# Three memsets of GpSimd between its indirect transfers, in a one-core kernel of a macaron network with a mixture of experts

## The chip, the core and the metric

The kernel runs on one core of a Trainium2 chip. A core has four engines that compute, each with its own queue of instructions that it works off in order: TensorE (PE in the profile; its weight loads are shown apart as PEld), VectorE (DVE), ScalarE (ACT) and GpSimd (POOL). SyncE (SP) issues plain DMA transfers. Transfers whose rows are picked by a list of indices (indirect transfers) are issued by GpSimd, which also makes their descriptors. Engines wait for each other through semaphores: an instruction counts one up when it is done, another waits until it has reached a value.

The metric is the time of one run on the device in microseconds. Three runs of the kernel before took 1364.46, 1364.88 and 1371.0 us; the median is 1364.88.

## What is computed

The reference has two layers around a stream `x` of four sequences of 512 positions with 128 features, all in fp32:

```python
x = L0_attn_x                                   # (4, 512, 128)
x = x + 0.5 * L0_ffn(layernorm(x))              # ternary-weight FFN, 512 hidden
x = x + L0_attn(layernorm(x))                   # a state-space recurrence (Mamba), 256 channels x 16 states
x = x + 0.5 * L0_ffn(layernorm(x))
x = x + 0.5 * L1_ffn(layernorm(x))              # mixture of experts: 64 experts, 8 for each row
x = x + L1_attn(layernorm(x))                   # causal attention, 8 heads, one key/value head
x = x + 0.5 * L1_ffn(layernorm(x))
```

The mixture of experts is what the change touches:

```python
rw = route(x)                                   # 8 experts of 64 for each row, with weights
expert_out = silu(x @ Wg[e].T) * (x @ Wu[e].T) @ Wd[e].T      # for every expert e
out = sum_e rw[:, e] * expert_out[e] + shared_mlp(x)
```

## The kernel before

**Stages.** The four sequences are called blocks. First come the two ternary FFNs and the recurrence of every block (about 400 us of the profile). Then follow the mixture of experts, attention, and the mixture of experts once more. In a mixture of experts two blocks form a group, and a group goes through three steps:

- *send* (L1065): the router picks 8 experts for each row. Every row is then written 8 times to the buffer `sent` in DRAM, sorted by expert. A scatter (L1147) writes one of the 8 copies of 128 rows of 512 bytes; a block takes 4 x 8 = 32 scatters (L1126 to L1128), a group 64.
- *by_tiles* (L1165): `sent` is read back in tiles of 128 rows that have one expert each, four tiles in a batch. TensorE transposes them, multiplies by the expert's weights, and SyncE writes the result to `back` in DRAM. 24 batches are always done; a rest that only some inputs need stands behind a branch (L1254), which all engines pass together.
- *take* (L1291): a gather (L1156) fetches one of the 8 results of 128 rows into a tile `y`. Again there are 32 in a block and 64 in a group. VectorE multiplies each by its weight and adds it to `total`. TensorE transposes the sum and VectorE adds it to `x`.

With four groups (two for each of the two mixtures) there are 256 scatters and 256 gathers. Two tiles `y` of 8 slices each are in use by turns, so a batch of gathers can run 16 ahead of VectorE.

**What sets the order.** Nothing is issued as the code is read. Every instruction is recorded as an `Op`, and a planner (`schedule`, L446) plays the engines through with costs for each instruction (`costs`, L380) and ranks, and puts out one order for each engine, which `issue` (L529) then writes out. For a scatter or gather the planner counts `INDIRECT` (L54) microseconds on GpSimd, and 6 more until the rows have landed (L418):

```python
        if op.name in ("scatter", "gather"):
            return INDIRECT, INDIRECT + 6.0
```

**What the change touches.** `issue` writes a small memset of GpSimd ahead of an operation that has the mark `apart`. Scatters have this mark (L1154): it says that scatters into the same buffer never write the same row, so that no wait is put between them. Gathers don't have it. The memset is `between` (L627), which writes 8 numbers of one partition of a tile `scratch` that nothing reads:

```python
    scratch = fixed.tile([1, 8], F32, tag="scratch", name="scratch")
    plan.between = lambda: real.gpsimd.memset(scratch, 0.0)
```

The planner doesn't know of these memsets; they are written out behind its back. Waits on semaphores are added by the framework, which sees that two memsets write the same tile.

Of the kernel before, what the change touches and what calls it, by code (L numbers as in the profile page):

```python
# [50 lines left out]
GROUPS = ((0, 1), (2, 3)), ((0, 1), (2, 3))  # L51
MOST = {n: ((n * S * TOPK + E * (P - 1)) // P + 3) // 4 * 4 for n in (1, 2)}
OFTEN = {2: 96, 1: 72}
INDIRECT = 1.25  # L54
READ = 4
PART = 11

# [221 lines left out]
class Plan:  # L279
# [100 lines left out]
    def costs(self, op):  # L380
# [36 lines left out]
        if op.name in ("scatter", "gather"):  # L417
            return INDIRECT, INDIRECT + 6.0  # L418
        if op.eng == "gpsimd":
# [26 lines left out]
    def schedule(self):  # L446
# [23 lines left out]
        while todo:  # L470
# [23 lines left out]
            t, op = best  # L494
            ready[op.eng].remove(op)
            issue, length = self.costs(op)
            if op.eng == "scalar":
                s = self.table(op)
# [8 lines left out]
            if op.eng == "tensor" and t > clock["tensor"] + 0.05:  # L507
                t += 0.1
            op.at, op.free_at, op.end = t, t + issue, t + length
            if op.eng == "sync":  # L510
                pipe = max(pipe, op.free_at) + length
# [17 lines left out]
    def issue(self, order):  # L529
        def real(x):  # L530
            return x.real() if isinstance(x, View) else x

        data = mybir.DependencyInfo(mybir.DependencyClass.Sync, mybir.DependencyReason.DATA)
        apart = {}

        def past(ins, op):
            for name in apart.get(op.past, ()):
                self.tc.add_manual_dep(ins.ins, name, data, reason="all rows")

        with self.tc.manual_schedule():  # L540
            for op in order:
                if op.go:
                    if op.apart:

                        self.between()
                    if op.name == "branch":
                        op.go(lambda ins: past(ins, op))
                        continue
                    ins = op.go()
                    if op.apart:  # L550
                        if op.apart in apart:
                            self.tc.declare_no_dep(ins.ins, group=op.apart, reason="no two rows are the same")
                        self.tc.add_to_no_dep_group(op.apart, ins.ins)
                        apart.setdefault(op.apart, []).append(ins.ins.name)
                    continue
                if getattr(op, "switch", False) and self.table(op) == "exp":
                    self.nc.scalar.preload_act_table_set("natural_log_exp_and_others")
                ins = getattr(getattr(self.nc, op.eng), op.name)(  # L558
                    *(real(x) for x in op.args), **{k: real(x) for k, x in op.kw.items()}
                )  # L560
                past(ins, op)
# [985 lines left out]
```

## Time and profile before

| | |
|---|---|
| median of three runs | 1364.88 us |
| the profiled execution, in whole | 1659.86 us |
| its span, on which all views of the profile stand | 1658.0 us |
| granted clock of TensorE in it | 0.856 |
| busy: PE, DVE, ACT, POOL | 1213.3, 986.4, 636.8, 550.2 us |
| 256 gathers on POOL (L1158) | 243.9 us, 953 ns each |
| 256 scatters on POOL (L1149) | 277.7 us, 1085 ns each |
| 256 memsets of `scratch` (L627) | 95 ns each at the median |

The profiled execution is 295 us longer than the runs that are timed; durations are read from it, and the time that counts is that of the runs. In a row of the timeline the first number is the start in us from the span's start, the second the length in us, then come engine, line, operation, what is written and read, and in brackets how long the engine had been idle and what ended that ("issue" is time in which it waited for nothing that the profile shows). Rows of an indirect transfer on POOL show the making of its descriptors; the landing of the rows is not in them. Operations that the planner writes out have the line of the helper that issues them (L558), so they are told apart by their tiles. In a table of windows each row has the stretch, its length, the busy time of each engine with its instructions, the granted clock, the share of the DMA engines and GB/s.

### The profile page before, as it was taken

The page shows a single profiled execution, that of the slowest core. Times are in us where ns is not written, and L with a number is a line of the kernel's source. Part 1 is how long each engine was busy: PE and PEld are TensorE (multiplying, and loading weights), DVE is VectorE, ACT ScalarE, POOL GpSimd, SP SyncE. Part 2 cuts the span into 40 slices and gives each one's busy share as a digit, 9 for nine tenths or more (in the row PEclk, how much of TensorE's full clock was granted, in tenths as well). Part 3 has the DMA queues.
Part 4 walks back from the last instruction along what each step waited for, and adds up shares of the span by engine and source line. Part 5 has one row for each costly group of instructions (what it writes and reads, how often), then busy time and mean ns, then how long its engine had stood idle before and what let it go on. Part 6 is the DMA issues. An engine that isn't in the chain of part 4 may idle for free. (4 is left out here: it accounts for less than half of the span.)

```text
span 1658.0 us, 17225 instructions
## 1 busy us (share of the span) xinstructions
PE 1213.3 (73%) x5006; PEld 740.8 (45%) x5006; DVE 986.4 (59%) x2413; ACT 636.8 (38%) x1207; POOL 550.2 (33%) x794
## 2 busy tenths in 40 slices
PE   6999989999897857567697686693964965676600
PEld 4743323334332436457574333351542655566500
DVE  1287899999896636335464567473674563254422
ACT  4776678674543332122243242251432512221200
POOL 0000000002865434434513554307044043345375
PEclk8999999999997978688797889797996986887855
DMA  4366847541306314334321110001011133344321
GB/s 142 103 224 225 277 161 203 185 116 32 87 23 223 110 62 132 92 122 132 115 90 40 38 36 29 26 4 61 7 37 40 39 110 106 121 130 120 117 59 47
DMA packets 74583, 166.72 MB, mean 101 GB/s; under 512 B 17688, under 2 KB 27953, under 8 KB 73361
## 3 DMA queue, kind: packets, MB, share of 16 engines
q1 hardware_dynamic: 58097, 131.89, 25.4%
q0 software_dynamic: 16384, 33.59, 6.7%
q8 instruction: 50, 0.82, 0.2%
q14 instruction: 52, 0.43, 0.1%
HBM read 117.44 MB, written 83.36 MB: 121 GB/s over the span
## 5 line engine op out<-in xcount | busy, mean ns | idle before, releaser
L1158 POOL DMA_INDIRECT y<-back,at x256 | 243.9, 953 | 329.4 <-issue 112.0
L1149 POOL DMA_INDIRECT sent<-xt,at x256 | 277.7, 1085 | 175.4 <-issue 79.4
L558 PE MATMUL bank<-h,h 128*128 128x512 f32 (+1 forms) x576 | 243.3, 565 | 8.5 <-DVE h L558 6.4
L1232 PE MATMUL bank<-gate_up,xc 128*128 x768 | 169.6, 350 | 47.9 <-DVE xc L558 14.6
L558 ACT ACTIVATE hr<-bank 128x176 f32<-128x176 f32 x192 | 59.3, 319 | 296.0 <-PE bank L1232 123.2
L558 PEld LDWEIGHTS bank<-h,h 128*128 128x128 f32 x576 | 108.7, 195 | 129.0 <-issue 112.8
L1232 PEld LDWEIGHTS bank<-gate_up,xc 128*128 128x128 f32 x768 | 136.0, 216 | 63.8 <-issue 31.0
L1232 PE MATMUL bank<-down,hc 88*128 x768 | 137.9, 295 | 27.3 <-DVE hr L558 13.8
L558 PE MATMUL ys<-pt,vo 128*128 128x512 f32 (+3 forms) x256 | 94.4, 488 | 79.7 <-ACT pt L558 56.7
L558 DVE TENSOR_TENSOR hr<-hr,bank 128x176 f32<-128x176 f32 x192 | 62.4, 332 | 133.1 <-ACT hr L558 79.5
L1232 PEld LDWEIGHTS bank<-down,hc 88*128 88x128 f32 x768 | 121.9, 207 | 35.2 <-DVE hr L558 17.0
L558 DVE TENSOR_TENSOR_SCAN hs<-da,hs 128x512 f32<-128x512 f32 (+1 forms) x128 | 132.1, 1074 | 0.2
L558 DVE COPY xc<-bank 128x512 f32<-128x512 f32 x96 | 65.8, 687 | 101.5 <-PE bank L558 58.3
L558 PE MATMUL bank<-ident,xr 128*128 128x128 f32 x384 | 88.7, 297 | 48.1 <-DMA xr<-sent 17.4
L558 ACT ACTIVATE p<-p,a_low 128x256 f32<-128x256 f32 (+3 forms) x128 | 70.8, 554 | 132.6 <-DVE a_low L558 95.7
L558 POOL MEMSET eq<- 128x256 f32 x8 | 2.6, 321 | 357.6 <-DVE gt L558 357.6
L558 PE MATMUL bank<-kt,q 128*128 128x512 f32 (+3 forms) x256 | 88.4, 470 | 39.9 <-DVE q L558 30.3
L558 ACT ACTIVATE h<-bank,vec 128x512 f32<-128x512 f32 (+1 forms) x108 | 67.2, 639 | 111.4 <-PE bank L558 102.7
L558 DVE SCALAR_TENSOR_TENSOR total<-y,by,total 128x128 f32<-128x128 f32 x224 | 77.5, 347 | 51.8 <-DMA y<-back,at 46.9
L558 DVE CUSTOM_DVE_ANT_0 p<-bank,mask 128x512 f32<-128x512 f32 (+3 forms) x128 | 58.9, 486 | 82.6 <-remote 47.6
L558 PEld LDWEIGHTS ys<-pt,vo 128*128 128x128 f32 x256 | 48.4, 208 | 118.0 <-ACT pt L558 64.2
L558 ACT ACTIVATE da<-rep,neg_a 128x512 f32<-128x512 f32 (+1 forms) x160 | 88.7, 625 | 26.5 <-DVE hs L558 24.9
(188 smaller groups left out, 2082.0 us busy)
## 6 DMA issues: line engine op xcount, KB each, us to landing
sent<-zero SPq DMA_DIRECT2D x48, 512.0 KB
xr<-sent SPq DMA_DIRECT2D x96, 256.0 KB
back<-yr SPq DMA_DIRECT2D x96, 256.0 KB
rep<-spread SPq DMA_DIRECT2D x48, 256.0 KB
back<-zero SPq DMA_DIRECT2D x14, 512.0 KB
bc<-kept SPq DMA_DIRECT2D x24, 256.0 KB
rep<-spread SPq DMA_DIRECT2D x32, 128.0 KB
sent<-xt,at POOLq DMA_INDIRECT x256
```

The source lines that it names most:

```text
L558: ins = getattr(getattr(self.nc, op.eng), op.name)(*(real(x) for x in op.args), **{k: real(x) for k, x in op.kw.items()})
L1149: return real.gpsimd.indirect_dma_start(out=rows.real(), out_offset=bass.IndirectOffsetOnAxis(ap=at.real(), axis=0), in_=x.real(), in_offs ...
L1158: return real.gpsimd.indirect_dma_start(out=y.real(), out_offset=None, in_=rows.real(), in_offset=bass.IndirectOffsetOnAxis(ap=at.real(), ...
L1232: return real.tensor.matmul(ps.real(), lhsT=lhs.real(), rhs=w.real()[..., bass.ds(to["at"][j] * n, n)], start=True, stop=True)
```

## The change

Scatters and gathers both get three memsets of `scratch` ahead of them, where scatters had one and gathers none. The planner's cost of an indirect transfer on GpSimd goes from 1.25 to 1.7 us. Since the planner makes the order of all engines from its costs, that order is made anew.

```diff
-INDIRECT = 1.25
+INDIRECT = 1.7
+PACE = 3
...
         with self.tc.manual_schedule():
             for op in order:
                 if op.go:
-                    if op.apart:
-
-                        self.between()
+                    if op.name in ("scatter", "gather"):
+
+                        for _ in range(PACE):
+                            self.between()
                     if op.name == "branch":
                         op.go(lambda ins: past(ins, op))
                         continue
```

## The prediction

> **What bounds the kernel now.** I read the profile from its end. The chain of work that ended last, in order of time, is one repeating pair: a gather on GpSimd (POOL, 0.94 us) and 0.30 us of "issue", until the last gather lands and VectorE adds its rows up. This is the window from 1627.76 us, with rows left out:
>
> ```profile
> 1627.76 0.95 POOL y L1158
> 1628.71 0.30 issue
> 1629.01 0.94 POOL y L1158
> ...
> 1631.51 2.43 DMA y<-back,at
> ...
> 1650.01 0.69 DVE x L558
> ```
>
> The reader is to see that nothing but GpSimd's issue sets the pace there. One landing of 2.43 us shows, once. POOL's own timeline shows where this tail begins, and what stands ahead of it:
>
> ```profile
> 1541.95 0.95 POOL L1158 DMA_INDIRECT y<-back,at  x1 [0.30 <-issue]
> 1567.75 0.94 POOL L1158 DMA_INDIRECT y<-back,at  x1 [24.85 <-SPq L1254]
> 1569.00 0.94 POOL L1158 DMA_INDIRECT y<-back,at  x1 [0.30 <-issue]
> ```
>
> The last batch of 64 gathers starts at 1567.75, after POOL sat idle for 24.85 us waiting for the branch at L1254 (it stands behind the last expert tiles). From start to start a gather takes 1569.00 - 1567.75 = 1.25 us, so the tail is 64 x 1.25 = 80 us. That whole tail is on the path; the other 192 gathers and 256 scatters are issued while TensorE has other work.
>
> A scatter in an undisturbed stretch, from the same view:
>
> ```profile
> 1240.68 0.09 POOL L627 MEMSET scratch<- 1x8 f32 x1
> 1240.98 0.97 POOL L1149 DMA_INDIRECT sent<-xt,at  x1 [0.21 <-issue]
> 1241.95 0.10 POOL L627 MEMSET scratch<- 1x8 f32 x1
> 1242.26 0.97 POOL L1149 DMA_INDIRECT sent<-xt,at  x1 [0.21 <-issue]
> ```
>
> A scatter has one memset ahead of it and a pitch of 1242.26 - 1240.98 = 1.28 us (1.27 at the median of most batches); a gather has none and 1.25. So the first memset costs 0.02 us: it lies inside the 0.30 us that POOL needs between two transfers anyway.
>
> **The change, part by part.** Removed: nothing. Added: scatters go from one memset to three (256 x 2 = 512), gathers from none to three (256 x 3 = 768). The constant moves only where the planner thinks the transfers end.
>
> *One chained memset.* In the built program's order every memset of scratch but the first waits for GpSimd's own count, because the one before writes the same tile. The trace never shows two of them in a row, so I bound the step. Near rows, from the start of POOL's timeline:
>
> ```profile
> 0.25 0.10 POOL L1540 MEMSET const-float32-0.0<- 128x1 f32 x1 [0.25 <-issue]
> 0.28 0.12 POOL L1540 MEMSET const-float32-1.0<- 128x1 f32 x1
> ...
> 1.07 0.20 POOL masks.py:65 MEMSET upper<- 128x128 f32 x1
> 1.32 0.29 POOL masks.py:199 TENSOR_SCALAR_AFFINE_SELECT ident<-ident 128x128 f32<-128x128 f32 x1
> ```
>
> Without a wait, memsets follow each other at 0.03 us. With a wait on POOL's own count (the select), the next starts 0.05 us after the end of the instruction before it (1.07 + 0.20 = 1.27). A memset of scratch lasts 0.095 us, so a step is 0.095 + 0.05 = 0.145 us. At the most each one pays the 0.21 us that a transfer pays after a memset: 0.305. The first of the three hides as today's does (0.02); two steps are added: for a gather 0.02 + 2 x 0.145 = 0.31 us at the near row, 0.63 at the upper end; 0.02 less for a scatter. At the lower end the transfer's 0.30 us of preparation overlaps the waits and about 0.1 is left. I take 0.35, close to the near row (the one measured wait of this kind on this engine) and leaning a little to the planner's own 1.7 - 1.25 = 0.45.
>
> *A rule against a row.* The Trainium skill, GPSIMD Engine Reference, section "Instruction dispatch", says that consecutive Pool instructions are no barrier: the next one starts before the one before has ended everywhere. By this rule three memsets stream at the 0.03 us of the constants' rows, 0.09 us in all, and vanish in the 0.30 us: the sum would be 1365. But the rule speaks of instructions without a semaphore wait between them, and these have one; the select's row decides, and by it the tail grows.
>
> *The tail.* 64 x 0.35 = 22.4 us, all of it on the path, since POOL is never idle there but for its 0.30 us. A second rule speaks against this cost: DMA: Bandwidth & Descriptors, section "Anatomy of one DMA", puts the fixed 2.0 us of such a transfer mostly in the write's receipt and little in its setup, so slower issue would hide under landings. By that, the tail grows by nothing. The row disagrees: landings overlap, the 2.43 us appear once at the end, and 64 pitches of 1.25 us make the length. I go by the row.
>
> *Everything else on POOL* has slack. The batch of gathers before the tail may end 24.85 us later before it delays the tail; it has 64 gathers, so 22.4 us: it fits, barely. The first layer's second batch of gathers ends at 995.7 and the next scatter starts at 1014.2: 18.5 us of slack, so those scatters start 3.9 us later. They and the following batch have 60 and 67 us of idle POOL behind them. The last scatters end at 1385.1, and POOL's next work comes 45.9 us later; 32 x 0.33 = 11 us fits. The first layer's scatters end at 522.4 and 684.7, with 34 and 42 us of slack behind them, against at most 21. Cover gone, this would cost up to 20 us at one place.
>
> *The planner.* It counts 1.7 where it counted 1.25, and so moves VectorE's sums of gathered rows behind more expert work. POOL's order is the same but for one mask memset that comes two scatters earlier. TensorE and VectorE change places of instructions from the first scatters on; no new transfer or queue entry arises. I give this 3 us for the batch that fits barely and either sign of 10 for the shuffle.
>
> **Sum.** 22.4 + 3 = 25 us. The profiled execution took 1659.86 us (span 1658.0), the runs 1364.88 at the median: it is 295 us longer than what is timed. Its own sum would be 1659.86 + 25 = 1685. I carry the 25 us unscaled to the median, as POOL's pitch is its own: 1390 us, 1.8% slower.
>
> **Rivals.** *Pacing frees the other engines (faster).* There are stretches where everything but POOL stands still while scatters run:
>
> ```profile
> core 0: us, PE busy (x) PEld busy (x) DVE busy (x) ACT busy (x) POOL busy (x), PEclk, DMA share, GB/s
> 1144.70:1158.30 13.60, 0.00 (x0) 0.00 (x0) 0.01 (x1) 0.00 (x0) 9.47 (x18) 0.50 0.14 48
> 1233.50:1256.70 23.20, 0.00 (x0) 0.00 (x0) 0.00 (x0) 0.02 (x1) 19.35 (x37) 0.56 0.16 54
> ```
>
> In the second, ScalarE waits 23.93 us for TensorE's count though the matmuls ended at 1232.5. Eight such stretches make 96.9 us. If half of that exists in the timed runs and gaps between transfers let the counts through, it gives 25 - 48 = -23: 1342. It decides from 25 us saved. Against it: these stretches already have a memset and 0.30 us between transfers, and the timed run is 295 us shorter than the profiled one, so most of the stalls can't be in it. Chance 0.10.
>
> *The memsets hide (no change).* The rule above holds and 0.30 us covers all three: 1365. For it: the first one hides. Against it: the wait on POOL's count. Chance 0.12.
>
> *A dear chain (much slower).* Each step is 0.305: the tail gains 64 x 0.63 = 40, the batch before it overruns its 24.85 by 15: 1420. Chance 0.13. For it: a transfer does pay 0.21 after a memset.
>
> **How the numbers follow.** Likeliest (0.65): 1390, its own range 1375 to 1405 from 0.2 to 0.5 us a gather and the shuffle. The range 1360 to 1420 takes in the hidden case and half of the dear one, and leaves out the faster case and the other half: 0.10 + 0.07. About 0.5% (7 us) is what a measurement of this kernel can tell from no change. Faster 0.10 (pacing), same 0.12, slower 0.65 + 0.13 = 0.78.
>
> **What would show it.** In the profile after: pairs of memsets of scratch 0.15 us apart from start to start; a gather pitch of 1.6 and a scatter pitch of 1.6; a last batch of 64 gathers some 100 us long at the end; idle before it shrunk from 24.85 to a few us. Wrong would be: memsets 0.03 apart (no change), steps of 0.3 (dear), or standing stretches gone and a shorter time (pacing).

## The result, and the profile after

The changed kernel takes **1409.47 us** (median of 4 runs, 1406.87 to 1409.97) against 1364.67 us before (4 runs, 1363.49 to 1371.0): a ratio of 1.0306 with an interval of 1.0287 to 1.0325, or 44.8 us more. The forecast was 1390 us and slower, its range 1360 to 1420. Sign and range hold; of the 44.8 us, the forecast had 25.

The profiled execution of the changed kernel took 1406.87 us, the same as its timed runs; the one of before had taken 1659.86 us, far from its own. The two traces can't be laid side by side to see what the change costs: before's is 253 us *longer*. The experiments show what that was (the second and third group below); the stages of the loss are therefore compared with the kernel of the second experiment instead.

The costliest groups of the page after that belong to the change (line, engine, operation, tiles, count, then busy us, mean ns of one, idle time ahead of them):

```profile
L1151 POOL DMA_INDIRECT sent<-xt,at x256 | 267.3, 1044 | 174.8 <-issue 105.2
L1160 POOL DMA_INDIRECT y<-back,at x256 | 245.3, 958 | 71.3 <-issue 37.7
L629 POOL MEMSET scratch<- 1x8 f32 x1536 | 150.4, 98 | 59.3
```

The transfers cost GpSimd what they did before. All that is new there is 1536 memsets instead of 256, with 59.3 us of idle time just ahead of them. (Lines are two further down than before.) GpSimd's timeline of the kernel after, at the last batch of gathers and inside it:

```profile
1289.49 0.95 POOL L1160 DMA_INDIRECT y<-back,at  x1 [0.15 <-issue]
1290.44 0.40 POOL L629 MEMSET scratch<- 1x8 f32 x3
1298.11 0.95 POOL L1160 DMA_INDIRECT y<-back,at  x1 [7.27 <-SPq L1256]
1299.06 0.40 POOL L629 MEMSET scratch<- 1x8 f32 x3
1299.61 0.95 POOL L1160 DMA_INDIRECT y<-back,at  x1 [0.15 <-issue]
...
1309.56 0.40 POOL L629 MEMSET scratch<- 1x8 f32 x3
1310.56 0.95 POOL L1160 DMA_INDIRECT y<-back,at  x1 [0.61 <-DVE total L560]
```

The three memsets end 0.40 us after the first starts. With 0.095 us for one that makes a step of (0.40 - 0.095) / 2 = 0.153 us. The next gather then starts 0.15 us later, so the pitch is 1299.61 - 1298.11 = 1.50 us (it was 1.25). The first gather into a tile `y`, each eighth, takes 0.46 us more. The last two rows show one. In the built program such a gather waits for two counts, VectorE's sums among them, and every other one for a single count.

### The profile page after: what moved, and what is told of

Its sections match the earlier page's. It is cut to its first block, busy times and chain, and to the rows that moved or that the text cites. A ratio compares the mean times of both kernels' runs of the same rounds, so it can differ in the third digit from the quotient of the medians.

```text
span 1405.1 us, 18486 instructions
## 1 busy us (share of the span) xinstructions
PE 1147.9 (82%) x5006; PEld 702.6 (50%) x5006; DVE 982.2 (70%) x2413; ACT 643.8 (46%) x1211; POOL 666.2 (47%) x2074
## 5 line engine op out<-in xcount | busy, mean ns | idle before, releaser
L1151 POOL DMA_INDIRECT sent<-xt,at x256 | 267.3, 1044 | 174.8 <-issue 105.2
L629 POOL MEMSET scratch<- 1x8 f32 x1536 | 150.4, 98 | 59.3
L1234 PE MATMUL bank<-gate_up,xc 128*128 x768 | 149.3, 322 | 3.7 <-DVE xc L560 2.0
L1234 PE MATMUL bank<-down,hc 88*128 x768 | 125.6, 282 | 7.1 <-DVE hc L560 5.6
L1234 PEld LDWEIGHTS bank<-gate_up,xc 128*128 128x128 f32 x768 | 121.2, 195 | 15.6 <-issue 8.3
L1234 PEld LDWEIGHTS bank<-down,hc 88*128 88x128 f32 x768 | 112.7, 196 | 12.4 <-DVE hc L560 4.2
L560 ACT ACTIVATE p<-p,a_low 128x512 f32<-128x512 f32 (+3 forms) x128 | 70.8, 554 | 91.8 <-DVE a_low L560 91.6
L560 PE MATMUL bank<-ident,total 128*128 128x128 f32 x32 | 9.2, 353 | 114.0 <-DVE total L560 113.9
L560 PE MATMUL bank<-kt,q 128*128 128x512 f32 (+3 forms) x256 | 82.9, 444 | 13.8 <-DVE q L560 9.0
L560 ACT COPY yr<-bank 128x512 f32<-128x512 f32 x96 | 56.1, 585 | 81.3 <-PE bank L1234 76.4
```

The costliest lines, as they stand in the source:

```text
L560: ins = getattr(getattr(self.nc, op.eng), op.name)(*(real(x) for x in op.args), **{k: real(x) for k, x in op.kw.items()})
L1151: return real.gpsimd.indirect_dma_start(out=rows.real(), out_offset=bass.IndirectOffsetOnAxis(ap=at.real(), axis=0), in_=x.real(), in_offs ...
L1234: return real.tensor.matmul(ps.real(), lhsT=lhs.real(), rhs=w.real()[..., bass.ds(to["at"][j] * n, n)], start=True, stop=True)
```

## The experiments

The experiments of a group ran side by side on one chip with the kernel before, so each group below has its own time of before (the third has two chips and two such times). After the result I held this: the gap that the wait adds to each transfer costs time in more places than the tail, and the new order gives a part of it back. The rivals were that the order itself is what costs, that the memsets cost as instructions and not by their waits, and that the loss lies in the tail alone.

### First group: one part alone (before 1365.36 us, 1363.55 to 1368.15, 14 runs)

**Memsets without the planner's new cost.**

```diff
-INDIRECT = 1.7
+INDIRECT = 1.25
```

> The three memsets of the changed kernel with the planner's old cost of 1.25 us. Theory A (the memsets are the cost: from the last scatters on, GpSimd is the bound in timed runs, so about 160 to 190 transfers pay 0.25 us each): 1365 + 40 to 48, near the changed kernel's 1409 or a little over. Theory B (only the last 64 gathers pay, 16 to 19 us, and the rest of the 45 us comes from the planner's new order): about 1383. In the profile a gather pitch of 1.50 us in either.

Measured: 1459.32 us, ratio 1.0684 (1.0665 to 1.0703). That is 94 us lost, twice the loss of the whole change and more than was expected.

**The planner's new cost without any added memset** (on the kernel before).

```diff
-INDIRECT = 1.25
+INDIRECT = 1.7
```

> The planner's cost of 1.7 us with the memsets of before (one ahead of a scatter, none ahead of a gather). Theory A: 1365 within 6 us, since the order alone costs nothing. Theory B: 1385 to 1392, since the new order carries some 25 us of the loss. Gather pitch 1.25 us.

Measured: 1349.41 us (1348.74 to 1350.14), ratio 0.9883 (0.9865 to 0.9901): 16 us gained. No kernel of this study is faster where before takes 1365 us; on the other kind of chip (second group) it was not run.

**One memset ahead of every transfer, old cost.**

```diff
-INDIRECT = 1.7
-PACE = 3
+INDIRECT = 1.25
+PACE = 1
```

> One memset ahead of scatters and gathers alike, planner's cost 1.25 us. Both theories: the memset lies inside the 0.30 us between two transfers (0.02 us each), so 1365 to 1369. It also asks what the profile of before did to its run: if it is a memset between gathers that lets the profiled execution run at its timed speed, this one's profiled execution takes about 1370 us; if it takes three, it takes about 1660 as before.

Measured: 1369.51 us, ratio 1.0027 (1.0017 to 1.0037), at a gather pitch of 1.26. A gather's first memset costs about 0.01 us, and 2 to 5 us come out at the end. This kernel has the planner's order of before, and so serves below as a trace of that order in an execution of 1372.02 us.

**Three memsets that don't wait for each other.** Nine tiles are used by turns, so that a memset doesn't write what the one before it wrote.

```diff
-    scratch = fixed.tile([1, 8], F32, tag="scratch", name="scratch")
-    plan.between = lambda: real.gpsimd.memset(scratch, 0.0)
+    scratch = itertools.cycle(
+        [fixed.tile([1, 8], F32, tag=f"scratch{i}", name=f"scratch{i}") for i in range(9)]
+    )
+    plan.between = lambda: real.gpsimd.memset(next(scratch), 0.0)
```

> The changed kernel with its three memsets in turn into nine tiles, so that none waits for the one ahead of it. If the waits between the memsets make their price (theory of the prediction): memsets 0.03 us apart, gather pitch 1.25 to 1.32, time that of the planner's change alone, 1365 to 1375. If a memset costs 0.15 us whether it waits or not: pitch 1.50 and 1409.

Measured: 1353.95 us (1351.01 to 1355.26), ratio 0.9913 (0.9889 to 0.9936). GpSimd's timeline of this run, in the last batch:

```profile
1282.15 0.17 POOL L631 MEMSET scratch<- 1x8 f32 x3
1282.47 0.95 POOL L1162 DMA_INDIRECT y<-back,at  x1 [0.15 <-issue]
1283.42 0.17 POOL L631 MEMSET scratch<- 1x8 f32 x3
1283.74 0.95 POOL L1162 DMA_INDIRECT y<-back,at  x1 [0.15 <-issue]
```

Three memsets take 0.17 us instead of 0.40, and the pitch is 1.27. The same number of instructions on the same engine, without the waits, costs 1353.95 - 1349.41 = 4.5 us; with them it costs 1409.47 - 1349.41 = 60.1. So it is the wait of one memset for the one before that is paid for, not the memset.

**What the four say together.** The order made with 1.7 is worth 16 us when the pitch is 1.25. At the pitch of 1.50, the planner that counts 1.25 loses another 50 us (1459.32 - 1409.47). VectorE shows where. It works off its queue in order, and the planner places the sums of gathered rows in that queue for the time at which it thinks the rows have landed. The view of who waited for whom (total us, times, longest), with the old cost and three memsets:

```profile
DVE total L560 <- DMA y<-back,at: 172.2, 154, 8.7
```

The same row with the old cost and one memset:

```profile
DVE total L560 <- DMA y<-back,at: 94.8, 96, 9.2
```

With three memsets VectorE stands 77 us longer in front of its sums, and all that is queued behind each sum stands with it. The end moves by 1459.8 - 1370.2 = 89.6 us of span. (How much of the 89.6 comes by way of these waits was not measured apart.)

### Second group: which transfers (before 1665.87 us, 1658.82 to 1670.1, 9 runs)

These were meant to tell which batches of transfers carry the cost. On this chip the kernel before took 300 us longer than in the first group, in timed runs.

**The kernel before, once more** (no edit).

> The kernel before, unchanged, profiled once more. If the standing stretches of its first profile belong to that one execution, this one takes about 1365 us under the profiler, and shows how much room really lay behind each batch of transfers: 10 us or less ahead of the last 64 gathers, in place of the 24.85 read before. If they belong to the kernel, it takes about 1660 us again.

Measured: 1663.85 us, and its trace has the standing stretches of the prediction's profile again. The table of windows, for the third batch of scatters of the second mixture (its columns are in the first line, each engine's instructions in brackets):

```profile
core 0: us, PE busy (x) PEld busy (x) DVE busy (x) ACT busy (x) POOL busy (x), PEclk, DMA share, GB/s
1228.30:1269.00 40.70, 8.39 (x44) 6.05 (x42) 10.65 (x38) 6.55 (x19) 34.03 (x63) 0.68 0.18 62
```

And the waits of the same stretch (from 1230 to 1270 us):

```profile
PEld ys L558 <- issue: 31.1, 1, 31.1
PE ys L558 <- issue: 30.8, 1, 30.8
ACT pt L558 <- remote: 30.3, 1, 30.3
```

GpSimd keeps its rhythm, while TensorE stands for 30.8 us, and VectorE and ScalarE with it; the stretch ends at 1268.5, during the last of the 32 scatters. TensorE has a wait there, though its row says "issue": its next matmul reads `pt`, and ScalarE and VectorE write `pt` from a `bank` that TensorE has filled. From the timeline of the same run:

```profile
1236.79 1.20 PE L558 MATMUL bank<-ident,p 128*128 128x128 f32 x8
1237.83 0.49 PE L558 MATMUL bank<-ident,xr 128*128 128x128 f32 x3
...
1268.52 0.58 ACT L558 COPY pt<-bank 128x512 f32<-128x512 f32 x1 [30.26 <-remote]
1269.16 2.08 PE L558 MATMUL ys<-pt,vo 128*128 128x512 f32 x2 [30.84 <-issue]
...
1270.57 0.69 DVE L558 COPY pt<-bank 128x512 f32<-128x512 f32 x1 [31.58 <-remote]
```

The matmuls into `bank` end by 1238.3, and both readers start 30 us later. "Remote" means that a count went up then though no instruction that raises it had just ended. In the packed trace this count is TensorE's own: its last update before the stretch comes at 1236.8 us, the next at 1268.4, while three matmuls that raise it end by 1238.3. So TensorE's work is done, and its count reaches the others late. Over this whole trace 105 of the 1201 recorded updates of that count come more than 1.5 us after the last matmul that raises it, but only 2 of VectorE's 1837 and 2 of ScalarE's 793; in the third experiment's trace it is 2 of TensorE's 1275. Waits ended by "remote" add up (over the engines) to 351 and 393 us in the two profiles of the kernel before, and to nothing in the four traces of the first group and in the changed kernel's of the result.

So the 1659.86 us of the first profile were no fault of that execution alone: on this chip the kernel takes that long in every timed run.

**Memsets in the last 64 gathers alone** (planner 1.7, one memset ahead of scatters).

```diff
+                        gathers += op.name == "gather"
-                        for _ in range(PACE):
+                        for _ in range(1 if op.name == "scatter" else PACE if gathers > 192 else 0):
```

> The planner's cost of 1.7 us (1349 us with the memsets of before), and three chained memsets ahead of the last 64 gathers alone. All of that batch is on the path: 64 x 0.25 and 0.45 more at each eighth, which waits for two counts: 19 us, so 1368. If the price is spread otherwise (the tail hides part behind landings), less than 1360.

Measured: 1656.27 us, ratio 0.9941 (0.9909 to 0.9973). It has the planner's new order as well and gains only 10 us, so the far larger gains of the next two are not that order's.

**Memsets ahead of scatters alone** (gathers have none).

```diff
-                        for _ in range(PACE):
+                        for _ in range(PACE if op.name == "scatter" else 0):
```

> Planner's cost 1.7, three memsets ahead of scatters, none ahead of gathers. By the room that the prediction read (34 to 46 us behind the batches of scatters) nothing: 1349. By the traces after (the experts' first tiles come directly behind the last scatters): 8 to 28 us, so 1357 to 1377.

Measured: 1470.11 us, ratio 0.8832 (0.8795 to 0.8869): 196 us *faster*.

**Memsets ahead of gathers alone** (scatters keep their one).

```diff
-                        for _ in range(PACE):
+                        for _ in range(PACE if op.name == "gather" else 1):
```

> Planner's cost 1.7, three memsets ahead of gathers, one ahead of scatters as before. By the prediction's room: the tail alone, 1368. By the traces after: the tail 19, the batch before it 16 to 18, the first mixture's up to 10: 1384 to 1396. With the scatters' run this should add up to the changed kernel's 60 us over 1349, if batches don't share room.

Measured: 1572.47 us, ratio 0.9441 (0.9409 to 0.9472): 93 us faster. On this chip each kind that is paced gives back standing time, most of all the scatters: the waits ended by "remote" come to 89 us with the scatters paced and 224 with the gathers.

### Third group: the change on such chips

**The changed kernel itself, once more** (no edit; before 1672.02 us here, 1665.89 to 1679.92, 12 runs).

> The changed kernel once more, beside the kernel before on the same chip. The kernel before took 1365 us on one chip and 1665 on another, so the chip decides what is tested. Where before takes 1365: 1409 again. Where before takes 1665 (its engines stand still while transfers are issued at 1.25 us): if the longer gap of the three chained memsets frees them, as it did for scatters and gathers alone (1470 and 1572), both together take 1400 to 1420; if part of the stalls stays, 1450 or more.

Measured: 1432.81 us (1430.5 to 1435.23), ratio **0.857** (0.8549 to 0.859). The same kernel that loses 44.8 us in the result gains 239 us here. The table of windows, for the same batch of scatters as above:

```profile
core 0: us, PE busy (x) PEld busy (x) DVE busy (x) ACT busy (x) POOL busy (x), PEclk, DMA share, GB/s
1058.50:1110.90 52.40, 45.64 (x216) 31.34 (x215) 40.96 (x129) 24.96 (x61) 41.19 (x125) 0.97 0.23 75
```

The batch is 11.7 us longer, and TensorE is busy for 45.64 us in it instead of 8.39, at a granted clock of 0.97 instead of 0.68. With the same planner's order on the same chip but unpaced scatters (the next run) it is busy for 14.37 us in this batch. The waits ended by "remote" come to 14.5 us in the whole trace.

**The tail alone, again** (the edit of the second group, on the chip of the run above).

> Planner's cost 1.7 and three memsets ahead of the last 64 gathers alone. Where before takes 1365, the planner's cost alone gives 1349 and the tail's price is 64 x 0.25 + 8 x 0.45 = 19 us: 1368. Where before takes 1665: 1656 again, as the tail has no other engine's work to free.

Measured: 1672.13 us, ratio 0.9996 (0.9966 to 1.0025), where the last chip had given 0.9941. With such differences between chips, the tail's price can't be read here; it is taken from traces below.

**The unchained memsets and the gathers alone, again** (the edits above; before 1674.56 us, 1672.46 to 1684.63, 7 runs).

> Planner's cost 1.7 and three memsets that don't wait for each other: as many memsets as the changed kernel has, but a gather pitch of 1.27 us, not 1.50. Where before takes 1365: 1354 again. Where before takes 1665: if it is the longer gap between transfers that frees the other engines, they still stand still here and it takes 1640 to 1670; if it is the memsets as such, whatever the gap, it takes 1355 to 1430.

> Planner's cost 1.7, three chained memsets ahead of gathers, one ahead of scatters. Where before takes 1365: by the room that the prediction read, the tail alone, 1349 + 19 = 1368; by the stages of the traces, the tail 19, the batches before it 16 to 18 and the first mixture's up to 10: 1384 to 1396. Where before takes 1665: 1572 again.

Measured: 1641.51 us, ratio 0.979 (0.975 to 0.983), with the unchained memsets; 1596.81 us, ratio 0.9529 (0.9487 to 0.9571), with memsets ahead of gathers. Three memsets that leave the pitch at 1.27 us for gathers and 1.29 to 1.30 for scatters bring little here: their trace has ten standing stretches of 3 to 6 us that the first group's trace of this kernel doesn't have, and 249 us of waits ended by "remote". So it is not the memset as such that frees the engines, but the chained one, with its longer gap between transfers.

**What is shown and what stays open.** On three chips the kernel before takes 1666 to 1675 us in timed runs. The standing time all but goes away when the pitch of the indirect transfers grows from 1.25 (gathers) and 1.27 (scatters) to 1.50 and 1.52 us, and what stands in it are late counts of TensorE. Why these counts are late while GpSimd issues transfers was not found out, nor whether a pitch between 1.30 and 1.50 us would do. In every run the longer gap came with GpSimd's waits for its own count, so the two are not told apart. Each chip was used once, so whether the chip or something else at that time makes the difference is not shown; and on which chip the first profile was taken is not on record. The tail alone, the scatters alone and the gathers alone never ran on a chip without the stretches.

## Why the prediction was right, and where not

All of this is for the result and the first group, where before takes 1365 us. The timed loss is made up as follows. The planner's new order gives 16 us (second experiment: 1365.36 to 1349.41). From there to the changed kernel it is 1409.47 - 1349.41 = 60.1, across two sets of runs whose times of before agree within 0.7 us; in the two spans, 1405.1 - 1346.9 = 58.2. Both kernels have the same planner's cost, so their traces compare stage by stage:

| stage | planner alone, us | after, us | later by |
|---|---|---|---|
| first scatter starts | 402.3 | 404.4 | 2.1 |
| scatters of the first group end | 523.5 | 531.9 | 8.4 |
| last scatter of the first mixture ends | 660.5 | 675.9 | 15.4 |
| gathers of the first mixture end | 865.3 | 888.3 | 23.0 |
| last 32 scatters start | 1118.5 | 1139.4 | 20.9 |
| they end | 1159.5 | 1189.1 | 29.6 |
| the next 64 gathers start | 1169.2 | 1190.5 | 21.3 |
| they end | 1251.4 | 1290.4 | 39.0 |
| the tail's 64 gathers start | 1259.1 | 1298.1 | 39.0 |
| the last gather ends | 1338.8 | 1397.0 | 58.2 |

**The chained memset: right.** The step was forecast at 0.145 us from the select's row and measures 0.153. What was added on top wasn't needed: after a memset the transfer starts after 0.15 us and not after 0.21 as before, so 0.25 us a transfer came out, where the near row gave 0.31 and 0.35 was taken. The pitch is 1.50 and 1.52, not 1.6. The "dear chain" of 0.305 a step is refuted.

**The rule against the row: right where it applies.** The Trainium skill (GPSIMD Engine Reference, "Instruction dispatch") says that consecutive Pool instructions are no barrier. Without the waits, memsets follow each other 0.04 us apart and all but vanish (1353.95 against 1349.41). With them they don't. The row decided the case, as the prediction had it.

**The tail: right.** 58.2 - 39.0 = 19.2 us against 22.4: from the first gather to the last, 63 x 0.25 = 15.75, and 7 x 0.45 = 3.2 for the gathers that open a tile `y`. The Trainium skill's fixed 2.0 us of a transfer (DMA: Bandwidth & Descriptors, "Anatomy of one DMA") read as cover would have made it nothing; by these 19.2 us, slower issue did not hide under landings.

**The other 39 us: this step failed.** It reads "Everything else on POOL has slack", and counted 3 us. Two things were wrong with it.

First, an idle stretch of GpSimd was taken for slack, though what ends it depends on the very transfers that go before. The 24.85 us ahead of the tail end at the branch. VectorE passes that branch in its order, and the profile of before tells what stands ahead of it there. VectorE's timeline of the kernel before, the window from 1541 us:

```profile
1550.55 0.34 DVE L558 SCALAR_TENSOR_TENSOR total<-y,by,total 128x128 f32<-128x128 f32 x1
1551.31 0.69 DVE L558 SCALAR_TENSOR_TENSOR x<-bank,x 128x512 f32<-128x512 f32 x1 [0.42 <-PE bank L558]
1551.92 0.68 DVE L558 COPY hc<-bank 88x512 f32<-88x512 f32 x1
...
1560.91 0.69 DVE L558 COPY hc<-bank 88x512 f32<-88x512 f32 x1 [0.65 <-PE bank L558]
```

The sum of the last gathers (`total`), its addition to `x`, and *after them* the last expert tiles (`hc`). If those gathers come later, the tiles behind them come later, and so does the branch: the gap moves and doesn't shrink. In the first experiment, with this same order of work, it is 20.6 us from the end of the last gather (20.23 behind the memsets), and 22.45 in the third, though the batch ends 72.9 us later (1332.4 against 1259.5).

In the changed kernel nothing but the sums is left there. VectorE's timeline of the kernel after:

```profile
1290.63 0.35 DVE L560 SCALAR_TENSOR_TENSOR total<-y,by,total 128x128 f32<-128x128 f32 x1 [1.23 <-DMA y<-back,at]
1292.06 0.35 DVE L560 SCALAR_TENSOR_TENSOR total<-y,by,total 128x128 f32<-128x128 f32 x1 [1.08 <-DMA y<-back,at]
1292.98 0.69 DVE L560 SCALAR_TENSOR_TENSOR x<-bank,x 128x512 f32<-128x512 f32 x1 [0.57 <-PE bank L560]
```

Each sum waits for its rows. In the waits of this batch's second half (1240 to 1299 us) that comes to

```profile
DVE total L560 <- DMA y<-back,at: 24.8, 24, 2.7
```

and in the planner's order alone, for the same half (1208 to 1260 us), to

```profile
DVE total L558 <- DMA y<-back,at: 4.6, 4, 1.6
```

So this batch is on the path with all of its gathers: 39.0 - 21.3 = 17.7 us, of which 64 x 0.25 = 16.0 is the pitch. The gap ahead of the tail stays as it was, 7.27 us against 7.65. The forecast had 3 us for this batch.

Second, the other slacks were read from an execution that stood still a good part of the time. In that trace 45.9 us of idle GpSimd follow the last scatters and 42 the scatters of the first mixture. GpSimd's timeline with the planner's cost alone, at those places (the first transfer after each, and the tail):

```profile
660.82 0.97 POOL L1158 DMA_INDIRECT y<-back,at  x1 [0.30 <-issue]
...
1169.20 0.97 POOL L1158 DMA_INDIRECT y<-back,at  x1 [9.66 <-SPq L1254]
...
1259.09 0.94 POOL L1158 DMA_INDIRECT y<-back,at  x1 [7.65 <-SPq L1254]
1260.34 0.94 POOL L1158 DMA_INDIRECT y<-back,at  x1 [0.31 <-issue]
```

The slack is 0.30 us at the first place and 9.66 at the second. In the old order without the standing time (third experiment) it is 7.3 and 10.4. The same two places in the kernel after:

```profile
677.53 0.98 POOL L1160 DMA_INDIRECT y<-back,at  x1 [1.24 <-issue]
...
1190.45 0.98 POOL L1160 DMA_INDIRECT y<-back,at  x1 [0.92 <-SPq L1256]
```

GpSimd works through without a pause, and the other engines wait for it: TensorE, VectorE and ScalarE stand together for 19.5 us from 660.5 and 9.5 from 1184.5 us, where the planner's cost alone has 10.1 and 8.1. The first mixture with its two groups loses 23 us by its last gather, 13.3 of them by its last scatter (15.4 - 2.1). The last 32 scatters, 8.7 us longer, did find cover: it is the 9.66 us that shrink to 0.92. The prediction's sentence "Cover gone, this would cost up to 20 us at one place" names the right price; it was paid at two, in the first mixture and in the batch ahead of the tail.

**The planner: counted at nothing between ±10, measured at -16.** With 1.7 the planner puts expert tiles ahead of the sums: the gap ahead of the tail goes from 22.45 us (third experiment) to 7.65, and the last scatters start 8.2 us earlier. That the larger cost makes this better order even where the pitch is 1.25 was seen, and not explained.

**The sum.** 19.2 + 39.0 - 16 = 42.2, and 44.8 measured; the rest is 1.9 between spans and medians (60.1 against 58.2) and 0.7 between the two times of before (1365.36 against 1364.67). By the prediction's terms: tail 22.4 was 19.2, the rest of POOL 3 was 39, the planner 0 was -16. That the time still lies in the range is in part luck: the two misses have opposite signs, and 58 us without the planner's 16 would have been 1423.

**The rival "pacing frees the other engines".** On the chip of the result it is wrong. On the three chips with the standing stretches it is right that gaps between transfers let the counts through, and its size is too small: it forecast 48 us freed, and the one that ran the changed kernel gained 239. The argument against it, that "most of the stalls can't be in" the timed runs since these are 295 us shorter, held for the timed runs at hand. It was no argument about the kernel: the profile of before shows what chips of the second kind show in every run (1659.86 us against 1658.82 to 1670.1 on one of them), and the same forecast for such a chip would have had the wrong sign. That these stretches "already have a memset and 0.30 us between transfers" was no obstacle either; 0.25 us more was enough there.

## What to carry to other kernels

An idle stretch of an engine is slack only if what ends it doesn't depend on the work ahead of it: follow the releaser (here a branch, behind VectorE's sums of the same gathers) before you hide a cost in it. Where the profiled execution is far longer than the timed runs, its idle times belong to something else; settle first whether that is the execution or the chip, since the sign of a change can hang on it. A planner's cost is worth trying by itself, apart from the instructions that it is said to describe: here the constant alone gained 1.2% on the first group's chip, and the pacing alone, uncounted, lost 6.8%.

## What the runs showed of the hardware

- The same program took 1365 us on the first group's chip and 1666 to 1675 us on three others. On those, while GpSimd issues indirect transfers every 1.25 to 1.30 us, TensorE's count reaches the engines that wait for it up to 30 us after its matmuls have ended, and all three stand. At a pitch of 1.50 to 1.52 us the changed kernel took 1433 us on one of them. Why is open.
- A chain of GpSimd memsets into one tile costs 0.153 us a step, into different tiles 0.04 us. Three unchained ones fit almost wholly into the 0.30 us between two indirect transfers (pitch 1.27 instead of 1.25); three chained ones add 0.25.
- A gather with waits for two counts starts 0.46 us later than one with a single wait (0.61 against 0.15), behind the same three memsets; without chained memsets ahead of it no such pitch is seen in the tail (at most 1.26 us with the planner's cost alone, 1.28 with unchained ones).
